# Prologue of a deformable-convolution, scan and mixture kernel: table of cells from a padded transpose, image loop unrolled

## The chip, the core and the metric

The kernel runs on one core of one Trainium2 chip. The metric is the device time of one execution in microseconds. A core has five engines with queues of their own: TensorE (PE, with its weight loads shown as PEld), VectorE (DVE), ScalarE (ACT), GpSimd (POOL) and SyncE (SP). SP, ACT and POOL also issue transfers, which run on 16 shared DMA engines.

## What is computed

The input x has 8 images of 128 channels and 64 x 64 pixels. Layer 0 normalises each image by groups of four channels, computes a 3x3 convolution with 27 outputs per pixel (nine dy, nine dx, nine masks), and samples the normalised image bilinearly at nine moved positions per pixel, weighted by the mask's sigmoid. A 128 x 128 product per tap follows.

```
om = _conv(gn(x), w_off, b_off)                 # 27 x 64 x 64 per image
dy, dx, m = om[:, :9], om[:, 9:18], sigmoid(om[:, 18:])
v = g(y0,x0)*(1-wy)*(1-wx) + g(y0,x0+1)*(1-wy)*wx + g(y0+1,x0)*wy*(1-wx) + g(y0+1,x0+1)*wy*wx
out = einsum('bckhw,ock->bohw', v * m, weight) + bias      # pixels outside the image count as 0
x = x + out
```

Layer 1 treats the pixels as 4096 tokens per image: a state-space scan over the tokens (state 256 x 256 per image) and a mixture of 8 experts with the top 2, both after a layer norm and both added to the input.

## The kernel before

The kernel has two parts. A prologue prepares tables in HBM; then a loop over the 4096 tokens of all 8 images together does everything else (sampling, projections, scan, experts). The change is in the prologue alone.

**Tables in HBM.** `table` has a row for each cell of each image. A cell is a 2 x 2 neighbourhood of pixels, of 65 x 65 per image (CELLS = 65), counting those that hang over the border; its row holds the 128 channels of its four pixels, 512 floats or 2 KB. A sample needs exactly one cell, so the main loop gathers one row per pixel and tap (line 578). `recs` holds for each pixel nine cell numbers and 36 weights. `xl` is a copy of x with a zero tail. `rz` (two of them, 8.8 MB each) holds a block structure for the scan's decays that must be zero where the loop writes nothing.

**prepare()** (lines 159 to 217) loads A, splits it in three bf16 parts, stores them in `adr`, and loads them back into `alhs` by 18 small DMAs on SP and 18 on ACT. It then clears both `rz` from a zeroed tile `zr` (lines 196 to 201), the tails of `xl` and `recs`, and the border rows and columns of the table (lines 208 to 217, 64 DMAs).

**images()** (line 228) sets up constants and runs a hardware loop `tc.For_i(0, NB, 1)` (line 268) whose body is **image()** (line 271). All engines and outstanding transfers meet at a barrier between two turns. One turn:

- loads the image into `xb` by eight DMAs, half on SP and half on ACT, with bn_stats on DVE for each, and stores it to `xl` from ACT's queue (277 to 283);
- averages over groups by two small matmuls and gets the reciprocal deviation, with a square root on ACT (287 to 298);
- writes the normalised image `xn` on DVE and copies it into the padded `xpad` (66 x 66) on POOL (305 to 314);
- transposes `xn` by 32 transposes on PE into PSUM, in 8 groups; ACT and DVE take turns to copy the groups to `xtok`, pixels on partitions (319 to 327). Each group is stored into the four corners of the cells by eight DMAs of 64 x 4 pieces of 512 bytes, SP for even image rows and ACT for odd ones (328 to 337): 64 DMAs per image, whose targets interleave in `table`;
- computes the offsets: 8 groups of 9 matmuls, 27 output partitions by 512 pixels each (341 to 351), bias on DVE into `om_t`, four transposes into `omp`, copy on ACT into `om` (352 to 359);
- computes the cell numbers and weights on DVE in some 30 operations of 128 x 288 (366 to 407), called the record chain below, and stores `recs` (408).

The pools `big` and `small` have one buffer per tile, `vp` three, and the PSUM pool `ps` two for each of its tags `pa` and `pb`. A scheduler orders the prologue's instructions on each engine at build time; each engine then works strictly in that order. A DMA instruction waits on its issuing queue for what it needs, and what stands behind it in the queue waits too.

**The main loop** (line 1106) runs 8 turns of 32 blocks in an order written out by hand. It gathers from `table`, so it starts when the prologue's stores have landed; the first thing of the main part to run on POOL is the memset of `zc` (line 450). In it, line 1020 contracts the state with 32-column weights that go to four column positions of PE in turn.

Of the kernel before, what the change touches and what calls it, by code (L numbers as in the profile page):

```python
# [37 lines left out]
PADW = IMG + 2  # L38
CELLS = IMG + 1
NCELL = CELLS * CELLS  # L40
DIN = 256
NH = 2
# [5 lines left out]
NCH = BL // CH  # L48
CT = CH * QI
GD = 14  # L50
NA = P // GD
NG = 2 * NA + 1
GCOL = (NG + 1) * CT
RROW = GD * GCOL
# [22 lines left out]
def kernel(  # L77
# [19 lines left out]
    nc = tc.nc  # L97
    NB = x.shape[0]
# [7 lines left out]
    ident = const.tile([P, P], FP, name="ident")  # L106
# [15 lines left out]
        out=wdelta_sb, in_=w_delta.rearrange("(k p) d -> p k d", p=P)  # L122
# [11 lines left out]
        out=ew_sb.rearrange("p (e c) -> p e c", e=NEXP),  # L134
        in_=expert_w.rearrange("e d c -> d e c"),
# [23 lines left out]
    def prepare():  # L159

        with tc.tile_pool(name="pre", bufs=1) as pre, tc.tile_pool(
# [45 lines left out]

            tab = table.rearrange("(b y x) (q c) -> b y x q c", x=CELLS, y=CELLS, q=4)
# [19 lines left out]
    def images():  # L228

        with ExitStack() as es:  # L230
# [32 lines left out]
            nc.sync.dma_start(out=woff_sb, in_=w_off)  # L263
            boff_sb = one.tile([27, 1], FP, name="boff_sb")
            nc.sync.dma_start(out=boff_sb, in_=b_off.unsqueeze(1))
            first = one.tile([P, 1], FP, name="first")
            nc.vector.memset(first, float(CELLS + 1))
            with tc.For_i(0, NB, 1) as b:  # L268
                image(b, big, small, vp, ps, gavg, basey, basex, woff_sb, boff_sb, first)

    def image(b, big, small, vp, ps, gavg, basey, basex, woff_sb, boff_sb, first):
        xb = big.tile([P, NPIX], FP, name="xb")
        src = x[bass.ds(b, 1)].rearrange("o c n -> c (o n)")
        stats = small.tile([P, 8, 6], FP, name="stats")
        for i in range(8):
            cols = slice(512 * i, 512 * i + 512)
            (nc.sync if i % 2 == 0 else nc.scalar).dma_start(
                out=xb[:, cols], in_=src[:, cols]
            )
            nc.vector.bn_stats(stats[:, i, :], xb[:, cols])  # L280
        nc.scalar.dma_start(
            out=xl[bass.ds(b, 1), :, :NPIX].rearrange("o c n -> c (o n)"), in_=xb
        )

# [14 lines left out]

        xpad = big.tile([P, PADW, PADW], FP, name="xpad")  # L300
        nc.gpsimd.memset(xpad[:, 0, :], 0.0)  # L301
# [3 lines left out]
        xn = big.tile([P, NPIX], FP, name="xn")  # L305
        for i in range(4):
            cols = slice(1024 * i, 1024 * i + 1024)
            nc.vector.tensor_scalar(
                xn[:, cols], xb[:, cols], gmean, grstd, ALU.subtract, ALU.mult
            )  # L310
            nc.gpsimd.tensor_copy(
                xpad[:, 1 + 16 * i : 17 + 16 * i, 1 : 1 + IMG],
                xn[:, cols].rearrange("p (y x) -> p y x", x=IMG),
            )


        tab = table.rearrange("(b y x) (q c) -> b y x q c", x=CELLS, y=CELLS, q=4)
        xtok = big.tile([P, NT, P], FP, name="xtok")
        for i in range(NT // 4):
            tp = ps.tile([P, 4, P], FP, tag="pa", name="tp")  # L320
            for k in range(4):
                t = 4 * i + k
                nc.tensor.transpose(tp[:, k, :], xn[:, P * t : P * t + P], ident)
            if i % 2 == 0:
                nc.scalar.copy(xtok[:, 4 * i : 4 * i + 4, :], tp)
            else:
                nc.vector.tensor_copy(xtok[:, 4 * i : 4 * i + 4, :], tp)
            for q in range(4):
                dy, dx = divmod(q, 2)
                for r in range(2):  # L330
                    y0 = 8 * i + r - dy + 1
                    (nc.sync if r == 0 else nc.scalar).dma_start(
                        out=tab[
                            bass.ds(b, 1), y0 : y0 + 7 : 2, 1 - dx : 1 - dx + IMG, q, :
                        ].rearrange("o y x c -> x (o y) c"),
                        in_=xtok[64 * r : 64 * r + 64, 4 * i : 4 * i + 4, :],
                    )


        om = big.tile([P, NT, 27], FP, name="om")  # L340
        for i in range(NT // 4):
            op = ps.tile([P, 512], FP, tag="pb", name="op")
            for tap in range(TAPS):
                kh, kw = divmod(tap, 3)
                nc.tensor.matmul(
                    op[:27, :],
                    woff_sb[:, tap, :],
                    xpad[:, 8 * i + kh : 8 * i + kh + 8, kw : kw + IMG],
                    start=(tap == 0),
                    stop=(tap == TAPS - 1),  # L350
                )
            om_t = vp.tile([27, 512], FP, name="om_t")
            nc.vector.tensor_scalar(om_t, op[:27, :], boff_sb, None, ALU.add)
            omp = ps.tile([P, 4, 27], FP, tag="pa", name="omp")
            for k in range(4):
                nc.tensor.transpose(
                    omp[:, k, :], om_t[:, P * k : P * k + P], ident[:27, :27]
                )
            nc.scalar.copy(om[:, 4 * i : 4 * i + 4, :], omp)

# [3 lines left out]
        def cell(base, lo, name):  # L364
# [20 lines left out]
        idxf = tmp("idxf")  # L385
        nc.vector.tensor_scalar(idxf, ylow, float(CELLS), first, ALU.mult, ALU.add)
# [21 lines left out]
        nc.sync.dma_start(  # L408
            out=recs[bass.ds(b, 1), :NPIX, :].rearrange("o (t p) x -> p (o t) x", p=P),
            in_=rec,  # L410
# [754 lines left out]
```

## Time and profile before

| what | value |
|---|---|
| median of 10 runs | 37964.98 us (37910.76 to 37986.14) |
| the profiled execution | 37936.39 us |
| its span, first to last instruction | 37934.7 us |
| granted TensorE clock, mean | 0.964 |
| busy share PE, DVE, ACT, POOL | 83%, 72%, 63%, 82% |
| memset of zc, after the last image | at 1686.56 us |
| table stores: SP queue, ACT queue | 256 and 256 DMAs, 128.0 KB each |
| row zeros (rz) | 2 DMAs of 8828.8 KB |
| PE line 345 (offsets) in one image | 144 records, 64.5 us busy |
| PE line 323 (transposes) in one image | 32 records, 6.9 us busy |

The shares of the whole span describe the main loop, which fills 95% of it. For a change in the prologue the stretches up to 1687 us have to be asked for by themselves. In the timeline, a line gives the start, the time, the engine (SPq and ACTq are their queues), the line of the kernel, the operation, what it writes and reads, and in brackets how long the engine had been idle and what ended that. A matmul in f32 shows as two records.

### The profile page before, as it was taken

Reading aid. Unit: us, or ns where it says so; the run is one execution under the profiler, and the core shown is the slowest. Engines: PE = TensorE matmul, PEld = TensorE weight load, DVE = VectorE, ACT = ScalarE, POOL = GpSimd, SP = SyncE. Lnnn points to the kernel's source line nnn. Section 1 sums busy time; section 2 is a strip of 40 time slices with the busy share of each in tenths; the row PEclk is TensorE's granted clock in tenths of the full one; section 3 lists DMA queues with packets and bytes.
Section 4 is the critical chain, followed back from the end, with each engine's and each line's share of the span. In section 5 each row is a group of like instructions: output and inputs, shape, how many; then the busy total and the mean of one; then the engine's idle time right before and its main releaser. Section 6 shows DMA issues by size and latency. Waiting matters only on the chain. (4 is left out here: it accounts for less than half of the span.)

```text
span 37934.7 us, 852122 instructions
## 1 busy us (share of the span) xinstructions
PE 31421.4 (83%) x324270; PEld 17742.7 (47%) x324270; DVE 27305.8 (72%) x35860; ACT 24041.9 (63%) x62725; POOL 31041.9 (82%) x14691
## 2 busy tenths in 40 slices
PE   3488888888888888888888888888888888888888
PEld 1144444444444444444444444444444444444444
DVE  1277777777777777777777777777777777777777
ACT  0166666666666666666666666666666666666666
POOL 0188888888888888888888888888888888888888
PEclk7799999999999999999999999999999999999999
DMA  3333333333333333333333333333333333333333
GB/s 88 76 105 105 102 105 104 104 105 105 104 102 105 104 104 104 104 105 103 105 103 104 104 104 106 101 106 106 105 103 104 105 105 104 106 102 103 105 105 99
DMA packets 4799915, 3906.86 MB, mean 103 GB/s; under 512 B 3351549, under 2 KB 4378966, under 8 KB 4536022
## 3 DMA queue, kind: packets, MB, share of 16 engines
q1 hardware_dynamic: 4529962, 3182.00, 29.6%
q0 software_dynamic: 185760, 608.85, 5.8%
q10 hardware_dynamic: 80072, 61.51, 0.6%
q8 instruction: 2532, 41.48, 0.5%
q14 instruction: 1589, 13.02, 0.1%
HBM read 3268.71 MB, written 582.10 MB: 102 GB/s over the span
## 5 line engine op out<-in xcount | busy, mean ns | idle before, releaser
L1000 POOL TENSOR_TENSOR mt<-et,ht 128x1024 f32<-128x1024 f32 x12288 | 28721.7, 2366 | 4728.5 <-ACT et L972 3435.9
L972 ACT ACTIVATE et<-bank 128x448 f32<-128x448 f32 (+1 forms) x40980 | 19926.6, 519 | 10775.4 <-PE bank L963 10457.7
L1008 DVE TENSOR_TENSOR ht<-mt,up 128x1024 f32<-128x1024 f32 x12288 | 14964.7, 1218 | 8791.7 <-PE ud L988 5499.3
L963 PE MATMUL bank<-rt,alhs 126*128 126x224 bf16 (+1 forms) x81960 | 12586.5, 254 | 2336.2 <-ACT et L972 2056.9
L963 PEld LDWEIGHTS <-alhs 126*128 126x128 bf16 x81960 | 6874.6, 99 | 7538.4 <-issue 6740.5
L1020 PE MATMUL yp<-mt,zc 128*32 128x256 f32 x98304 | 9081.9, 394 | 0.0
L988 PE MATMUL up<-uu 32*128 32x256 bf16 x49152 | 4988.4, 274 | 1972.2 <-DVE ht L1008 1935.4
L1010 DVE TENSOR_TENSOR ud<-md,ud 128x1024 f32<-128x1024 f32 x4096 | 5004.0, 1222 | 0.0
L1000 DVE TENSOR_TENSOR md<-et,ud 128x1024 f32<-128x1024 f32 x4097 | 4973.6, 1214 | 22.3 <-ACT et L972 22.3
L1020 PEld LDWEIGHTS yp<-mt,zc 128*32 128x32 f32 x98304 | 3409.6, 111 | 2790.3 <-issue 1361.1
L1020 PE MATMUL yp<-md,zc 128*32 128x256 f32 x32768 | 4650.9, 406 | 0.0
L988 PEld LDWEIGHTS <-uu 32*128 32x128 bf16 x65536 | 1789.0, 92 | 5057.6 <-issue 4427.7
L611 PE MATMUL bank<-ident,w 128*128 128x128 f32 x18576 | 3142.5, 292 | 344.8 <-ACT et L972 220.9
L601 ACT ACTIVATE w<-g,rec 128x128 f32<-128x128 f32 x9288 | 3197.2, 404 | 128.9 <-DMA rec<-recs 113.2
L611 PEld LDWEIGHTS bank<-ident,w 128*128 128x128 f32 x18576 | 2429.5, 191 | 1138.3 <-ACT et L972 542.6
L578 POOL DMA_INDIRECT g<-table,rec x2322 | 2261.5, 974 | 498.3 <-issue 245.5
L988 PE MATMUL ud<-uu 32*128 32x256 bf16 x16384 | 1605.2, 273 | 361.4 <-DVE md L1000 351.2
L1020 PEld LDWEIGHTS yp<-md,zc 128*32 128x32 f32 x32768 | 1688.6, 113 | 0.0
L896 ACT ACTIVATE se<-bank,gate 128x128 f32<-128x128 f32 x2048 | 696.2, 367 | 539.0 <-PE bank L889 486.7
L301 POOL MEMSET xpad<- 128x66 f32 x8 | 1.2, 153 | 1226.9 <-POOLq L268 1226.8
L554 PE MATMUL bank<-wconv_sb,vt 128*128 128x128 f32 x4644 | 905.8, 295 | 0.0
L554 PE MATMUL bank<-ident,se 128*128 128x128 f32 x4096 | 821.6, 306 | 0.0
(200 smaller groups left out, 16369.8 us busy)
## 6 DMA issues: line engine op xcount, KB each, us to landing
rt<-rz SPq DMA_DIRECT2D x2050, 1102.5 KB
uu<-pr SPq DMA_DIRECT2D x8196, 36.0 KB
pr<-dpt SPq DMA_DIRECT2D x3084, 48.0 KB
pr<-bpt SPq DMA_DIRECT2D x3084, 48.0 KB
rz<-dst SPq DMA_DIRECT2D x6939, 21.0 KB
g<-table,rec POOLq DMA_INDIRECT x2322, 3.5
rec<-recs SPq DMA_DIRECT2D x2064, 2.8 KB
table<-xtok SPq DMA_DIRECT2D x256, 128.0 KB
```

The costliest lines, as they stand in the source:

```text
L554: nc.tensor.matmul(ps_out, lhs, rhs, start=(i == 0), stop=(i == n - 1))
L578: nc.gpsimd.indirect_dma_start(out=g, out_offset=None, in_=table, in_offset=bass.IndirectOffsetOnAxis(ap=rec.bitcast(I32)[:, j : j + 1], a ...
L601: nc.scalar.activation(ws[j][:, P * q : P * q + P], g[:, P * q : P * q + P], AF.Copy, scale=rec[:, c0 : c0 + 1],)
L611: nc.tensor.matmul(wk[:, :P], w[:, P * q : P * q + P], ident, start=(q == 0), stop=(q == 3),)
L896: nc.scalar.activation(se[:, ex, :], wk[:, P * j : P * j + P], AF.Copy, scale=gate[:, ex : ex + 1],)
L963: nc.tensor.matmul(ps[:, m * (NH * f + h) : m * (NH * f + h + 1)].rearrange("p (q t) -> p q t", q=n), alhs[:KR, g + f, P * h : P * h + P], ...
L972: nc.scalar.activation(ec[:, :, :, P * f + d0 : P * f + d0 + n], ps[:, m * f * NH : m * (f + 1) * NH].rearrange("p (h d t) -> p h t d", h= ...
L988: nc.tensor.matmul((up if p < QP else ud)[:, r, h], uu[c % 2][rows, 0, b % 2, lo, P * h : P * h + P], uu[c % 2][rows, 1, b % 2, lo, :], st ...
L1000: (nc.gpsimd if p < QP else nc.vector).tensor_tensor(buf(j, p), et[c % 2][:, lo, PAIRS[p][0] : PAIRS[p][1] + 1 : 2], ht[p] if p < QP else ...
L1008: nc.vector.tensor_tensor(ht[p], buf(j, p), up, ALU.add)
L1010: nc.vector.tensor_tensor(ud, buf(j, p), ud, ALU.add)
L1020: nc.tensor.matmul(yp[32 * (b // 2) : 32 * (b // 2) + 32, :DIN], zc[c % 2].rearrange("p s x -> p (s x)")[:, s0 : s0 + 32], buf(j, p)[:, r, ...
```

## The change

- **Loop.** The images are unrolled: image() is called eight times with a number in place of a register, so the scheduler sees all eight and there is no barrier between them. `first`, a running offset of the cell number, becomes a constant per image.
- **Table.** The normalised image goes straight into `xpad` (two buffers now); `xn`, `xtok` and POOL's copy are gone. For each of 66 padded rows and both dx, 65 pixels are transposed on PE, so that a tile `xc` of 65 partitions (cell columns) holds for 14 padded rows the pixel pairs. Two rows that follow each other in a partition are one cell, so 13 rows of cells are stored by one DMA with an overlapping source, in pieces of 2 KB: five DMAs per image, three on SP and two on POOL. The border cells come from the padding, so their zeroing goes. An image takes 140 transposes and 35 copies of 65 x 512.
- **Offsets.** Four groups of rows go to output partitions 0, 32, 64 and 96 of one PSUM bank, tap by tap; the bias has four copies; the later transposes read at the four offsets.
- **Row zeros.** `rz` is cleared from POOL's queue by eight DMAs of 112 rows of 10 KB behind each of the first two images, from a smaller zero tile set by POOL.

```diff
+CROW = 13
...
-            zr = pre.tile([GD * 8, 9 * RROW + GCOL // 8], BF, name="zr")
-            nc.vector.memset(zr, 0.0)
-            for k in range(2):
-                nc.sync.dma_start(
-                    out=rz[k].rearrange("q (r x) -> (q r) x", r=8), in_=zr
-                )
...
-            for b in range(NB):
-                for q in range(4):
-                    dy, dx = divmod(q, 2)
-                    nc.sync.dma_start(
-                        out=tab[b, dy * IMG, :, q, :], in_=zf[:CELLS, :P]
-                    )
-                    nc.scalar.dma_start(
-                        out=tab[b, :, dx * IMG, q, :], in_=zf[:CELLS, :P]
-                    )
...
-            with tc.For_i(0, NB, 1) as b:
-                image(b, big, small, vp, ps, gavg, basey, basex, woff_sb, boff_sb, first)
+            nz = (9 * NCH * RROW + GCOL) // 64
+            zr = one.tile([GD * 8, nz], BF, name="zr")
+            nc.gpsimd.memset(zr, 0.0)
+            for b in range(NB):
+                image(b, big, small, vp, ps, gavg, basey, basex, woff_sb, boff_sb)
+                if b < 2:
+                    for m in range(8):
+                        nc.gpsimd.dma_start(
+                            out=rz[b].rearrange("q (r m x) -> (q r) m x", r=8, m=8)[:, m],
+                            in_=zr,
+                        )
...
-        xpad = big.tile([P, PADW, PADW], FP, name="xpad")
+        xpad = big.tile([P, PADW, PADW], FP, name="xpad", bufs=2)
...
             nc.vector.tensor_scalar(
-                xn[:, cols], xb[:, cols], gmean, grstd, ALU.subtract, ALU.mult
-            )
-            nc.gpsimd.tensor_copy(
                 xpad[:, 1 + 16 * i : 17 + 16 * i, 1 : 1 + IMG],
-                xn[:, cols].rearrange("p (y x) -> p y x", x=IMG),
+                xb[:, 1024 * i : 1024 * i + 1024].rearrange("p (y x) -> p y x", x=IMG),
+                gmean, grstd, ALU.subtract, ALU.mult,
             )
...
+        for i in range(CELLS // CROW):
+            xc = vp.tile([P, CROW + 1, 2, P], FP, name="xc")
+            for j in range((CROW + 1) // 2):
+                tp = ps.tile([P, 2, 2, P], FP, tag="pa", name="tp")
+                for k in range(2):
+                    for dx in range(2):
+                        nc.tensor.transpose(
+                            tp[:CELLS, k, dx, :],
+                            xpad[:, CROW * i + 2 * j + k, dx : dx + CELLS], ident,
+                        )
+                dst = xc[:CELLS, 2 * j : 2 * j + 2]
+                if j % 2 == 0:
+                    nc.scalar.copy(dst, tp[:CELLS])
+                else:
+                    nc.vector.tensor_copy(dst, tp[:CELLS])
...
+            rows = bass.AP(
+                tensor=rows.tensor, offset=rows.offset,
+                ap=[rows.ap[0], (2 * P, CROW), (1, 4 * P)],
+            )
+            r0 = NCELL * b + CROW * CELLS * i
+            (nc.sync if i % 2 == 0 else nc.gpsimd).dma_start(
+                out=table[r0 : r0 + CROW * CELLS, :].rearrange("(y x) c -> x y c", x=CELLS),
+                in_=rows,
+            )
...
-        for i in range(NT // 4):
+        for i in range(2):
             op = ps.tile([P, 512], FP, tag="pb", name="op")
             for tap in range(TAPS):
                 kh, kw = divmod(tap, 3)
...
+                for g in range(4):
+                    y0 = 32 * i + 8 * g + kh
+                    nc.tensor.matmul(
+                        op[32 * g : 32 * g + 27, :], woff_sb[:, tap, :],
+                        xpad[:, y0 : y0 + 8, kw : kw + IMG],
+                        start=(tap == 0), stop=(tap == TAPS - 1),
+                    )
...
+            for g in range(4):
+                nc.vector.tensor_scalar(
+                    om_t[32 * g : 32 * g + 27], op[32 * g : 32 * g + 27],
+                    boff_sb[32 * g : 32 * g + 27], None, ALU.add,
+                )
...
-        nc.vector.tensor_scalar(first, first, float(NCELL), None, ALU.add)
```

On the queues, as the changed kernel is scheduled: ACT's 18 loads of alhs stand ahead of the first image's square root; on SP an image's record store and the loads of the next image's `xb` stand ahead of the next image's table stores; on POOL six of the rz stores stand ahead of the first table store; on DVE and ACT the statistics of the next image and its copy to `xl` stand between the copies out of PSUM; on PE an image's first matmul stands behind the last `omp` of the image before, and on DVE its normalisation behind the record chain of the image before.

More of the change, by code (lines that the diff above doesn't have):

```diff
@@ L206, in prepare @@
                 nc.scalar.dma_start(out=recs[b, NPIX:, :], in_=zf[: 2 * BL, :REC])
-            tab = table.rearrange("(b y x) (q c) -> b y x q c", x=CELLS, y=CELLS, q=4)
-            for b in range(NB):
-                for q in range(4):
-                    dy, dx = divmod(q, 2)
-                    nc.sync.dma_start(
-                        out=tab[b, dy * IMG, :, q, :], in_=zf[:CELLS, :P]
-                    )
-                    nc.scalar.dma_start(
-                        out=tab[b, :, dx * IMG, q, :], in_=zf[:CELLS, :P]
-                    )
     def rstd_of(pool, var, shape, eps, name):
@@ L263, in images, with image @@
             nc.sync.dma_start(out=woff_sb, in_=w_off)
[L264 to L268, printed above, removed]
-                image(b, big, small, vp, ps, gavg, basey, basex, woff_sb, boff_sb, first)
-    def image(b, big, small, vp, ps, gavg, basey, basex, woff_sb, boff_sb, first):
+            boff_sb = one.tile([P, 1], FP, name="boff_sb")
+            nc.vector.memset(boff_sb, 0.0)
+            for g in range(4):
+                nc.sync.dma_start(
+                    out=boff_sb[32 * g : 32 * g + 27], in_=b_off.unsqueeze(1)
+                )
[10 more added lines that the diff above has]
+                        )
+    def image(b, big, small, vp, ps, gavg, basey, basex, woff_sb, boff_sb):
         xb = big.tile([P, NPIX], FP, name="xb")
-        src = x[bass.ds(b, 1)].rearrange("o c n -> c (o n)")
         stats = small.tile([P, 8, 6], FP, name="stats")
@@ L277, in image @@
             (nc.sync if i % 2 == 0 else nc.scalar).dma_start(
-                out=xb[:, cols], in_=src[:, cols]
+                out=xb[:, cols], in_=x[b, :, cols]
             )
             nc.vector.bn_stats(stats[:, i, :], xb[:, cols])
-        nc.scalar.dma_start(
-            out=xl[bass.ds(b, 1), :, :NPIX].rearrange("o c n -> c (o n)"), in_=xb
-        )
+        nc.scalar.dma_start(out=xl[b, :, :NPIX], in_=xb)
         mv = small.tile([P, 2], FP, name="mv")
@@ L304, in image @@
         nc.gpsimd.memset(xpad[:, 1 : PADW - 1, PADW - 1], 0.0)
-        xn = big.tile([P, NPIX], FP, name="xn")
         for i in range(4):
-            cols = slice(1024 * i, 1024 * i + 1024)
             nc.vector.tensor_scalar(
-                xn[:, cols], xb[:, cols], gmean, grstd, ALU.subtract, ALU.mult
-            )
-            nc.gpsimd.tensor_copy(
-                xpad[:, 1 + 16 * i : 17 + 16 * i, 1 : 1 + IMG],
-                xn[:, cols].rearrange("p (y x) -> p y x", x=IMG),
-            )
@@ L317, in image @@
-        tab = table.rearrange("(b y x) (q c) -> b y x q c", x=CELLS, y=CELLS, q=4)
-        xtok = big.tile([P, NT, P], FP, name="xtok")
-        for i in range(NT // 4):
[L320 to L337, printed above, removed]
+                xpad[:, 1 + 16 * i : 17 + 16 * i, 1 : 1 + IMG],
@@ new lines, in image @@
+                xb[:, 1024 * i : 1024 * i + 1024].rearrange("p (y x) -> p y x", x=IMG),
+                gmean, grstd, ALU.subtract, ALU.mult,
+            )
+        for i in range(CELLS // CROW):
[13 more added lines that the diff above has]
+                    nc.vector.tensor_copy(dst, tp[:CELLS])
+            rows = xc[:CELLS, :CROW]
+            rows = bass.AP(
+                tensor=rows.tensor, offset=rows.offset,
+                ap=[rows.ap[0], (2 * P, CROW), (1, 4 * P)],
+            )
+            r0 = NCELL * b + CROW * CELLS * i
[3 more added lines that the diff above has]
+            )
@@ L340, in image @@
         om = big.tile([P, NT, 27], FP, name="om")
-        for i in range(NT // 4):
+        for i in range(2):
             op = ps.tile([P, 512], FP, tag="pb", name="op")
@@ L344, in image @@
                 kh, kw = divmod(tap, 3)
[L345 to L350, printed above, removed]
-                )
[L352 to L359, printed above, removed]
+                for g in range(4):
[5 more added lines that the diff above has]
+                    )
+            om_t = vp.tile([P, 512], FP, name="om_t")
+            for g in range(4):
+                nc.vector.tensor_scalar(
+                    om_t[32 * g : 32 * g + 27], op[32 * g : 32 * g + 27],
+                    boff_sb[32 * g : 32 * g + 27], None, ALU.add,
+                )
+            for g in range(4):
+                omp = ps.tile([P, 4, 27], FP, tag="pa", name="omp")
+                for k in range(4):
+                    nc.tensor.transpose(
+                        omp[:, k, :], om_t[32 * g : 32 * g + 27, P * k : P * k + P],
+                        ident[32 * g : 32 * g + 27, 32 * g : 32 * g + 27],
+                    )
+                t0 = 16 * i + 4 * g
+                nc.scalar.copy(om[:, t0 : t0 + 4, :], omp)
         def tmp(name):
@@ L385, in image @@
         idxf = tmp("idxf")
-        nc.vector.tensor_scalar(idxf, ylow, float(CELLS), first, ALU.mult, ALU.add)
+        nc.vector.tensor_scalar(
+            idxf, ylow, float(CELLS), float(NCELL * b + CELLS + 1), ALU.mult, ALU.add
+        )
         nc.vector.tensor_add(idxf, idxf, xlow)
@@ L408, in image @@
         nc.sync.dma_start(
-            out=recs[bass.ds(b, 1), :NPIX, :].rearrange("o (t p) x -> p (o t) x", p=P),
+            out=recs[b, :NPIX, :].rearrange("(t p) x -> p t x", p=P),
             in_=rec,
```

## The prediction

> **What bounds the kernel now.** The profiled execution took 37936.39 us (span 37934.7); the median of the ten runs is 37964.98, 28.6 more. The sum is made against the profiled one and 28.6 is added at the end. A tenth of a per cent or two (the runs span 75 us) is all that a measurement of this kernel can tell from no change, hence the bound of 0.2% below.
>
> I read the table by stretches first. Up to 1.69 ms the profile shows another program: PE busy 37%, ACT 4%.
>
> ```profile
> 300.00:500.00 200.00, 74.56 (x212) 23.25 (x212) 30.51 (x60) 7.56 (x16) 5.94 (x8) 0.67 0.30 68
> 1300.00:1500.00 200.00, 74.47 (x212) 23.16 (x212) 33.72 (x65) 7.56 (x16) 5.95 (x8) 0.67 0.32 76
> 1900.00:2100.00 200.00, 166.50 (x1746) 92.51 (x1739) 152.21 (x211) 133.01 (x345) 174.28 (x83) 0.98 0.40 109
> ```
>
> Columns: stretch, length, busy us of PE, PE weight loads, DVE, ACT, POOL (instructions), granted clock, DMA share, GB/s. In the image loop no engine is half busy and DMA is at 0.30. So a wait bounds it: next come the waits of the SP queue in 0 to 1700 us (total us, times, longest) and the timeline of one image.
>
> ```profile
> SPq L332 <- DMA table<-xtok: 1112.3, 312, 5.5
> SPq L332 <- ACT xtok L325: 91.8, 8, 14.1
> SPq L268 <- DMA recs<-rec: 85.2, 8, 11.0
> ```
>
> ```profile
> 325.01 0.15 POOL L301 MEMSET xpad<- 128x66 f32 x1 [173.76 <-POOLq L268]
> 338.30 2.91 PE L323 MATMUL tp<-ident,xn 128*128 128x128 f32 x12 [1.53 <-DVE xn L308]
> 340.06 165.40 SPq L332 DMA_DIRECT2D table<-xtok  x32
> 414.41 0.46 DVE L367 TENSOR_TENSOR posy<-om,basey 128x288 f32<-128x288 f32 x1 [1.01 <-ACT om L359]
> 424.76 0.69 DVE L407 TENSOR_TENSOR rec<-posy,posx 128x288 f32<-128x288 f32 x1
> 1492.73 0.15 POOL L301 MEMSET xpad<- 128x66 f32 x1 [176.03 <-POOLq L268]
> 1673.15 0.44 SPq L408 DMA_DIRECT2D recs<-rec  x1
> 1686.56 1.95 POOL L450 MEMSET zc<- 128x1088 f32 x2 [175.08 <-DMA table<-xtok]
> ```
>
> Six images lie between 325.01 and 1492.73: 194.6 us each. 165.4 of it is the train of table stores: 32 on SP and 32 on ACT, each waiting for the one before (2.6 us a store), at 50 GB/s. Arithmetic ends at 425.5, 100 us into the image; the rest is the train and the loop's barrier. The scan begins when everything before it is done (1686.56) and lasts 36,248 us.
>
> **The change, part by part.** After the prologue the order of the instructions is the same on every engine, so those 36,248 us stay. What moves is 1686.56, rebuilt from three pieces.
>
> *Start, now 130 us.* Out go the memset of zr (16.88 us on DVE), the row zeros that held all DMA engines from 25 to 80 us, and 64 border stores (111.5 to 129). The 18 loads of alhs on each queue stay; SP took 15.29 us for its own undisturbed, ACT 37.7 under the row zeros. ACT's stand ahead of the first image's square root. adr can land by about 20 us, 18 loads at SP's 0.85 make 35, plus normalisation: transposes from 38. Bounds 30 (0.55 a load, ACT's median issue) and 70 (2.1, as now).
>
> *Eight images.* The train becomes five stores of 845 pieces of 2 KB (1.73 MB), none of which waits for another; xc has three buffers. SP issues three, POOL two. Bytes stay at 8.65 MB an image. What the stores cost on the engines is bounded by rows: the 2 KB loads of xb ran at 406 GB/s (21 us an image), the 512-byte border stores at 150 (58 us). I take 26, nearer to the row with the same piece size. With xb and xl (2.1 MB each, about 5 us each) and recs (about 9) transfers need 45 us an image.
>
> ```profile
> 330.00:332.00 2.00, 0.00 (x0) 0.00 (x0) 1.89 (x3) 0.00 (x0) 0.00 (x0) 0.50 1.05 406
> ```
>
> That is below the arithmetic, which now sets the period. PE's order lets an image start only after the last omp of the one before, and DVE puts the whole record chain between that and the next normalisation. One image:
> - record chain, 414.41 to 425.45: 11.0.
> - dev to the first transpose (335.71 to 338.30): 2.6.
> - 35 tiles of 4 transposes (140 for 32 before), each evicted by ACT (0.585) or DVE (0.69) from two banks, with 18 rounds of four offset matmuls between. Now two tiles and two matmul records take 2.0 us (152.60 to 154.60: eight transposes 1.09, two records 1.04). A round is eight records on four column sets; if they overlap it is 2 x 0.43, so again 2.0 a pair: 17.5 x 2.0 = 35.
> - xb has one buffer: the next load starts after the normalisation, and bn_stats on DVE and the xl store on ACT wait for it ahead of evictions, and those hold up PE. Load 8 us (326 to 334), queued beside recs, so landing about 18 us after the chain, when some 8 tiles (10.6 us) are done: 7.
> - clock: after the chain it is 0.50 and eight transposes took 1.75 for 1.09; a pair then costs 3.8, two pairs until it is warm, once more after the stall: 7.
> - DVE in order: four om_t of 0.74 ahead of an eviction, twice, less what two banks cover: 4.
> - eight omp with evictions at the end, 0.7 each: 5.5.
>
> Sum 72 us. Bounds: 51 (PE dense, no stall) and 96 (cold throughout). Costed at nothing: POOL's copies to xpad (5.4, gone), the memsets of xpad, POOL's issue of two stores (0.95 for 128 pieces of a gather, so some 6 each; behind them only memsets that are needed an image later), 8 bn_stats in the load's shadow.
>
> Do the column sets overlap? Line 1020 of the scan does the same, 32 columns at four positions:
>
> ```profile
> 20002.34 0.73 PE L963 MATMUL bank<-rt,alhs 126*128 126x224 bf16 x4
> 20003.00 1.07 PE L1020 MATMUL yp<-mt,zc 128*32 128x256 f32 x16
> 20004.00 0.56 PE L963 MATMUL bank<-rt,alhs 126*128 126x224 bf16 x4
> ```
>
> 16 records of 256 columns in 1.07 us; one by one at 0.43 per 512 columns they would take 3.4. So 64.5 us of offsets become about 16. Without it an image costs 48 more.
>
> The Trainium skill (TensorEngine Tiling (Array Packing), Key Properties) says that changing the tiling mode drains TensorE. The kernel now alternates transposes on the whole array with rounds on column sets 36 times an image. The trace above switches both ways with neighbours overlapping, so no drain shows. Were it to cost a matmul's tail (0.379 less 0.213 us, 0.17) each time, it would add 6 us an image, and the forecast would be 36,960.
>
> *Row zeros*, 17.7 MB at the 340 GB/s of 30 to 70 us: 52 us of all engines, in 16 POOL stores, now beside images 0 and 1. Those two need 90 of 144 us for their own, so together they just fit; POOL's own table store stands behind six of them in its queue, and a late one holds an xc buffer. I take 10, bounds 0 and 52.
>
> *End*: recs store to barrier, 1673.15 to 1686.56: 13. Most rec loads are then done early: 3 us less.
>
> Sum: 38 + 8 x 72 + 10 + 13 = 637, for 1686.6. Saved 1050 + 3; 37936.4 - 1053 = 36,883, and 28.6 more for the median: **36,910**.
>
> **Rivals.**
> 1. *Transfers become the bound.* With stores at 150 GB/s an image needs 58 + 19 = 77, and with stalls in bursts (three buffers, SP's stores behind rec loads that wait for recs) some 95: 8 x 23 more, 37,095. For: DMA at 0.55 when the 65-row stores ran at 150. Against: those are 32.5 KB each, on small pieces. The Trainium skill (DMA: Bandwidth & Descriptors, "How many engines (k)") says that a transfer uses the largest k up to 16 that divides its outer size; 65 rows would use 13, by which 406 becomes 330 GB/s and the stores 26 us. No run here shows the engines one by one. Chance 0.22.
> 2. *Column sets run one after another*: 120 an image, 37,295. Line 1020 speaks against it. 0.03.
> 3. *More overlap*: no stall, warm clock, 55 an image, 36,775. PE's order and the single xb are against it. 0.10.
> 4. *Slower: POOL's stores.* They are made of 845 pieces by an engine whose only transfers here are gathers of 128. If a piece costs much more in a store than there, two stores in a row set the image. The gather's landing, 3.6 us for 128, is 28 ns a piece: 24 us a store, 48 an image, hidden. It decides on the total from about 203 us an image (8 x 203 + 61 = 1686), that is 120 ns for each of 1690 pieces; at 150 ns it gives 254 an image, 38,375. Nothing in the trace comes near. 0.03.
> 5. *The change does not do what it says*: the new stores still wait for each other, 5 x about 8 us: 40 an image, hidden again; the time stays. It joins the forecast.
>
> **How the numbers follow.** Forecast 0.62 (36,800 to 37,020 by itself), rivals 0.22, 0.03, 0.10, 0.03. The range takes half of rival 3 and nearly all of rival 1: 36,780 to 37,160 (its top is 96 an image, start 70, zeros 52 less a little). Faster by over 0.2%: all but rival 4, less 0.01 for what I have not thought of, 0.96; slower 0.03; same 0.01.
>
> **What would show it.** Right: zc's memset near 640 us; image starts about 72 apart; SP's waits on its own table stores gone; the offset matmuls about 16 us busy an image; DVE waiting for xb some 7 us an image; DMA share near 0.6 in the images. Wrong: evictions waiting for a table store (rival 1), offset matmuls near 64 us (2), POOL transfers landing after more than 50 us (4), a start beyond 70, or a scan that is not 36,248 us within 0.2%.

## The result and the profile after

The change was faster: 36911.29 us median of 8 runs (36878.97 to 36929.18) against 37942.94 of 28 runs (37883.32 to 38005.75), ratio 0.9726 with a 95% interval of 0.9718 to 0.9735. The profiled execution took 36907.24 us, its span is 36902.8, and its memset of `zc`, which marks the end of the prologue, stands at 658.30 (line 452 now) instead of 1686.56. The scan behind it took 36902.8 - 658.3 = 36244.5 us, for 36248.1 before. So the whole gain, 1028 us, lies in the prologue.

The table by stretches, changed kernel, first the prologue as a whole and then the middle of the image loop (columns as before: length, busy us of PE, PE weight loads, DVE, ACT, POOL, granted clock, DMA share, GB/s):

```profile
0.00:658.00 658.00, 369.61 (x2564) 191.42 (x2564) 294.49 (x569) 134.44 (x259) 41.73 (x80) 0.80 0.80 200
300.00:500.00 200.00, 135.09 (x946) 68.66 (x946) 105.35 (x201) 46.39 (x91) 7.07 (x18) 0.80 0.85 200
```

Where DMA stood at 0.30 and 68 GB/s it now stands at 0.85 and 200. PE is at two thirds. So the DMA engines have less idle time left than any other engine, and the experiments ask what a byte more costs there.

The waits of the SP queue, 0 to 700 us:

```profile
SPq L328 <- DVE xc L319: 257.7, 21, 36.4
...
SPq L565 <- DMA recs<-rec: 61.0, 8, 28.8
```

The wait of a table store for a table store, 1112.3 us before, is not in the list. SP now waits for DVE to finish a tile, which is where it should wait.

The timeline, cut to the time around image 0 and to the end of the last image:

```profile
36.61 2.98 DVE L298 TENSOR_SCALAR xpad<-xb,gmean,g_r 128x1024 f32<-128x1024 f32 x4
36.74 3.99 POOL L261 DMA_DIRECT2D rz<-zr  x6 [0.30 <-POOL zr L256]
...
67.99 44.26 SPq L328 DMA_DIRECT2D table<-xc  x3
...
96.68 0.58 ACT L317 COPY xc<-tp 65x512 f32<-65x512 f32 x1 [21.83 <-DMA table<-xc]
...
112.31 26.83 SPq L271 DMA_DIRECT2D xb<-in_x  x4
...
166.40 2.71 DVE L274 BATCH_NORM_STATS2 stats<-xb 128x6 f32<-128x512 f32 x4 [34.23 <-DMA xb<-in_x]
...
582.15 2.98 DVE L298 TENSOR_SCALAR xpad<-xb,gmean,g_r 128x1024 f32<-128x1024 f32 x4
...
646.11 0.40 SPq L410 DMA_DIRECT2D recs<-rec  x1
...
658.30 1.95 POOL L452 MEMSET zc<- 128x1088 f32 x2 [42.53 <-DMA recs<-rec]
```

An image's time, or period, is counted below from the start of its normalisation to the start of the next one's. The eight images start their normalisation (line 298) at 36.61, 172.17, 235.51, 310.25, 380.37, 446.67, 514.76 and 582.15. Image 0 takes 135.6 us; the next six take 68.3 on average (410.0 / 6), the last 64.0 to its record store, and 12.2 follow. In image 0 the evictions wait 22 us for a table store and the statistics of image 1 wait 34 us for its load: those are the two places to ask about.

### The profile page after: what moved, and what is told of

Same layout as the page of the kernel before. It is cut to its first block, busy times and chain, and to the rows that moved or that the text cites. A ratio compares the mean times of both kernels' runs of the same rounds, so it can differ in the third digit from the quotient of the medians.

```text
span 36902.8 us, 851327 instructions
## 1 busy us (share of the span) xinstructions
PE 31218.1 (85%) x325134; PEld 17758.9 (48%) x325134; DVE 27338.0 (74%) x35939; ACT 24109.2 (65%) x62853; POOL 31010.2 (84%) x14692
## 5 line engine op out<-in xcount | busy, mean ns | idle before, releaser
L603 ACT ACTIVATE w<-g,rec 128x128 f32<-128x128 f32 x9288 | 3197.2, 404 | 43.8 <-DMA g<-table,rec 41.8
L556 PEld LDWEIGHTS bank<-wconv_sb,vt 128*128 128x128 f32 x4644 | 657.1, 190 | 263.4 <-issue 263.1
```

The lines of the kernel that those rows point to most:

```text
L556: nc.tensor.matmul(ps_out, lhs, rhs, start=(i == 0), stop=(i == n - 1))
L603: nc.scalar.activation(ws[j][:, P * q : P * q + P], g[:, P * q : P * q + P], AF.Copy, scale=rec[:, c0 : c0 + 1],)
```

## The experiments

The kernel before took 38419.49 us on the chip of the first four runs (7 runs; its granted clock there was 0.954 to 0.955, elsewhere 0.963 to 0.966), 37987.03 on that of the next four (one run) and 37929.1 on that of the last four (9 runs). So totals are compared as ratios, and prologues by the memset of `zc` in the profile.

### e1_zeros_last and e2_zeros_spread: the zeros moved in the text

```diff
-                if b < 2:
-                    for m in range(8):
...
+                if b == NB - 1:
+                    for k in range(2):
+                        for m in range(8):
...
```

That is e1, with all 16 stores behind the last image; e2 has two behind each image:

```diff
-                if b < 2:
-                    for m in range(8):
...
+                for m in range(2 * (b % 4), 2 * (b % 4) + 2):
...
```

> All 16 stores of row zeros stand behind the last image instead of eight behind each of the first two. In the changed kernel image 0 lasts 135.6 us and images 1 to 7 on average 67.7. Theory (the row zeros hold the DMA engines while image 1's load and image 0's table stores need them): image 0 takes 68 to 80 us, images 1 to 7 stay at 65 to 70, and the memset of zc, now at 658.3, comes at about 658 - 60 + 52 = 650, because the 52 us of zeros are then bare at the end. Rival (image 0 is long for its own reasons: cold clock, loads of alhs, first load of x): image 0 stays at 125 to 136 us and zc moves out to about 710.

> Two stores of row zeros (2.2 MB) behind each of the eight images. Theory (the zeros cost what they cost because 17.7 MB come at once): image 0 takes 68 to 80 us; each image carries 6.5 us more of transfers, of which the slack of some 7 us in a period of 67.7 hides most; periods of 67 to 73, zc at 595 to 630, total 30 to 60 us below the changed kernel. Rival A (image 0 long for its own reasons): image 0 at 125 to 136, zc at 655 or later. Rival B (transfers already bind, so bytes cost the same wherever they stand): periods of 74 or more, zc at 650 to 660, nothing gained.

Image 0 took 120.0 us in the first and 123.6 in the second; `zc` came at 650.9 and 654.8. The second, timed, had the ratio 0.973 (0.9714 to 0.9746), the same as the change. Read alone, that would have killed the theory. But POOL's timeline of the first shows that hardly anything had moved:

```profile
36.76 4.03 POOL L262 DMA_DIRECT2D rz<-zr  x6 [0.30 <-POOL zr L256]
...
70.46 1.07 POOL L262 DMA_DIRECT2D rz<-zr  x2
...
119.86 4.16 POOL L262 DMA_DIRECT2D rz<-zr  x8
```

The scheduler issues a store as soon as it is ready, wherever the program's text has it. The stores of zeros depend on nothing but their tile, so they went to the front in the order of the changed kernel; only the last eight came some 13 us later, from 119.86 on for 106.71. Neither run tells what zeros at another place would cost. They were repeated with the order pinned (below).

### e3_one_column_set: the offsets as before, the rest of the change kept

```diff
-        for i in range(2):
+        for i in range(NT // 4):
...
-                for g in range(4):
-                    y0 = 32 * i + 8 * g + kh
-                    nc.tensor.matmul(
-                        op[32 * g : 32 * g + 27, :], woff_sb[:, tap, :],
...
+                nc.tensor.matmul(
+                    op[:27, :], woff_sb[:, tap, :],
+                    xpad[:, 8 * i + kh : 8 * i + kh + 8, kw : kw + IMG],
...
```

> The offsets go back to eight groups of nine matmuls on one column set, the rest of the change stays. Theory (TensorE's work sets the period of an image and column sets take 43 us out of it): offsets 64.5 us busy an image instead of 21, periods of 105 to 115 us, zc at about 658 + 8 x 43 = 1000, total about 37,250. Rival (the transfers, 60 of 67 us, set the period): the longer matmuls hide partly, periods of 75 to 95, zc below 900.

Images 1 to 6 took 110.1 us (220.21 to 880.85, six periods) and `zc` came at 1002.0. The table by stretches:

```profile
500.00:600.00 100.00, 80.87 (x284) 29.74 (x283) 34.41 (x69) 15.44 (x28) 2.36 (x6) 0.88 0.52 116
```

The DMA share falls to 0.52 and PE is at 81%: the period follows TensorE's work, and column sets save 110.1 - 68.3 = 41.8 us an image. In the image from 441.39 to 550.68 the offset matmuls were busy for 68.3 us, in the changed kernel for 21.3, so only some 5 of these 47 us were hidden. TensorE in the changed kernel, where transposes of the table and offset matmuls take turns:

```profile
106.20 1.09 PE L311 MATMUL tp<-ident,xpad 128*65 128x128 f32 x8
...
107.22 1.06 PE L341 MATMUL op<-xpad,woff_sb 128*27 128x512 f32 x8
...
108.21 1.09 PE L311 MATMUL tp<-ident,xpad 128*65 128x128 f32 x8
```

Eight offset records, which one by one at 0.43 would take 3.4 us, take 1.06 on four column sets, and the whole turn takes 2.0.

### e4_old_unrolled: the old body, only unrolled

```diff
-            with tc.For_i(0, NB, 1) as b:
-                image(b, big, small, vp, ps, gavg, basey, basex, woff_sb, boff_sb, first)
+            for b in range(NB):
+                image(b, big, small, vp, ps, gavg, basey, basex, woff_sb, boff_sb, first)
```

> The image body, the border stores and the row zeros of before, but unrolled over the images in place of the hardware loop. Theory (the train of 64 table stores that wait for each other sets an image; the loop's barrier and the bare load are what unrolling takes out): 165 to 172 us an image for 194.6, zc at about 130 + 8 x 168 + 13 = 1490, total about 37,740. Rival 1 (unrolling is the main gain, and the chained waits came from the loop's form): below 120 us an image, zc below 1100. Rival 2 (nothing from unrolling, because the train of an image and the load of the next share the queues): 190 or more, zc at 1650 to 1690.

This is the run that changed the picture. `zc` came at 925.8: unrolling alone saved 1686.6 - 925.8 = 760.8 us of the 1028. The total was 37652.34 (one run, ratio 0.980). The seven periods average 97.0 us. SP's waits from 0 to 1800 us:

```profile
SPq L332 <- DMA table<-xtok: 10.0, 31, 1.0
```

and one image's stores in the timeline:

```profile
532.78 34.81 SPq L332 DMA_DIRECT2D table<-xtok  x32
```

SP's stores of 512-byte pieces, which waited 1112 us for table stores in the hardware loop, wait 10 us here, and SP issues the 32 of an image in 35 us instead of 165. The train was not a property of the stores: in an unrolled body, with a number for the image in their addresses, the waits are gone; in the hardware loop, with a register there, they are there (e5 shows the same for the new stores). Loop and register were changed together in both runs. That the build can compare only numbers for overlap is the likely reason, and it is not shown; the runs show the effect. The theory had expected the train to stay; rival 1 was right.

### e5_new_in_loop: the other half alone

```diff
-            for b in range(NB):
...
+            with tc.For_i(0, NB, 1) as b:
...
-                out=table[r0 : r0 + CROW * CELLS, :].rearrange("(y x) c -> x y c", x=CELLS),
+                out=cells[bass.ds(b, 1), CROW * i : CROW * i + CROW].rearrange("o y x c -> x (o y) c"),
```

> The new image body in the hardware loop of before, with a register for the image in every address; all row zeros behind the loop. The unrolled old body showed that its stores no longer wait for each other (10 us in all, for 1112). Theory (it is the register in the address, not the many small stores, that chains them): the five stores of an image wait one for the other again, each about 10 us from issue to landing, so that SP or POOL waits for table stores some 30 to 50 us an image, and an image takes 100 to 125 us, with the barrier and the bare load. zc at about 37 + 8 x 112 + 52 + 13 = 1000. Rival (the new stores are free of each other in any form): no such waits, and an image takes 85 to 95 us (67.7 with 8 of load, 12 of records and barrier bare), zc at about 37 + 8 x 90 + 65 = 820.

`zc` at 813.9, images 90.1 us apart, total 37022.68 (one run, ratio 0.975). The start was 75.2: image 0 is loaded inside the loop here, from 56.7 on, and the scheduler put half of the zeros ahead of the loop. The waits of SP and POOL, 0 to 650 us:

```profile
SPq L332 <- DMA table<-xc: 298.9, 13, 23.4
...
POOL table L332 <- DMA table<-xc: 66.4, 2, 33.5
```

The mechanism is the theory's: behind a register the new stores wait for each other again, 23 us at a time on SP. The price is the rival's: 90.1 us an image, so most of the chain must lie beside the arithmetic. Fewer, larger stores made the chain cheap; the unrolled loop, with numbers for addresses, made it go away.

### e10_old_table_columns: the loop and the offsets of the change, without its table and its row zeros

e4 with the offsets of the changed kernel (lines 335 to 360 there) in place of its own.

> The old image body unrolled, as in the fourth run, and the offsets on four column sets; the table stored as before by 64 stores of 512-byte pieces. In the fourth run an image took 97 us, with the offsets 64.5 us of TensorE and the transfers at a share of 0.55, some 54 us. Theory (unrolling and column sets are the gain, the new table form is not): 97 - 43 = 54 us of arithmetic with 54 us of transfers, stalls between them, 60 to 72 us an image; first normalisation at 142 as there, zc at about 142 + 7 x 66 + 70 = 675. Rival (the new table form is needed: 64 stores on two queues hold up the evictions on ACT and the transfers): 85 us an image or more, zc above 800.

Normalisations at 143.32, 201.71, 268.74, 333.34, 401.40, 466.74, 531.69 and 597.26: 64.8 us an image, averaged over seven. `zc` at 666.4, total 36901.42 (one run, ratio 0.971). With a start that is 107 us later than the changed kernel's it ends its prologue only 8 us later. The late start is the old one: the row zeros are issued from 24.67, the border stores from 111.38, and the images begin behind both. So what the change does to table and row zeros gave the early start and, with four column sets, hardly anything else. The four runs with numbers for addresses make a square (its first row also has the row zeros where they were before):

| `zc` at (first normalisation at) | one column set | four column sets |
|---|---|---|
| old table | 925.8 (142.6) | 666.4 (143.3) |
| new table | 1002.0 (37.7) | 658.3 (36.6) |

On one column set `zc` even comes 76 us later with the new table, in spite of the early start: an image takes 110.1 us for 97.0, and its 140 transposes keep TensorE busy for 22 us where the 32 old ones took 6.7.

### e1b_zeros_pinned_last and e2b_zeros_pinned_spread: the zeros really moved

```diff
+                    tc.keep_in_program_order(nc.gpsimd.dma_start(
                         out=rz[...].rearrange("q (r m x) -> (q r) m x", r=8, m=8)[:, m],
                         in_=zr,
+                    ))
```

> The row zeros pinned behind the last image's stores in POOL's order. (In the first two runs the scheduler had put six of the 16 ahead of the first table store, two behind it and eight behind image 0, whatever the text said, as in the changed kernel.) Theory (the zeros make image 0 long): image 0 at 68 to 85 us, images 1 to 7 at 65 to 70, zc at 635 to 660, the zeros bare at the end. Rival (image 0 is long for its own reasons: loads of alhs ahead of the table stores on SP, cold clock): image 0 at 115 or more, zc at 690 or later.

> Two stores of row zeros pinned behind the table stores of each image in POOL's order. Theory (the zeros' 52 us of transfers cost that much because they come at once; 6.5 us fit into an image's slack of some 7): image 0 at 70 to 85 us, the others at 67 to 72, zc at 590 to 625. Rival A (transfers bind, so that every byte costs its time anywhere): periods of 74 or more, zc at 645 to 665, as in the changed kernel. Rival B (image 0 long for its own reasons): image 0 at 115 or more, zc at 640 or later.

| zeros | image 0 | images 1 to 6, mean | last normalisation to `zc` | `zc` |
|---|---|---|---|---|
| ahead and beside images 0, 1 (the change) | 135.6 | 68.3 | 76.1 | 658.3 |
| all behind image 7 (e1b) | 82.5 | 69.7 | 139.1 | 678.9 |
| two behind each image (e2b) | 90.6 | 74.6 | 89.3 | 666.5 |

The theory on image 0 held: without the zeros it takes 82.5, so the zeros cost 53 us there. Its hope for a free place did not. Behind the last image they cost 63; spread, they cost 4.9 to 6.3 us in each period (74.6, for 69.7 in e1b or 68.3 in the change), with 2.2 MB of transfers added, 6.5 us at 340 GB/s. That is rival A of the second run, though `zc` came 1.5 us after the end of its range. The end of e1b in the table by stretches:

```profile
600.00:700.00 100.00, 16.09 (x95) 14.63 (x95) 14.64 (x33) 15.82 (x55) 20.45 (x25) 0.57 0.76 219
620.00:650.00 30.00, 0.00 (x0) 0.00 (x0) 0.00 (x0) 0.00 (x0) 2.62 (x5) 0.50 0.98 299
```

PE 16%, DMA 0.76 over a stretch that includes the first 21 us of the scan; from 620 to 650 no other engine than POOL works, and the zeros move with the last of the image's stores. They go in pieces of 10 KB, at 299 GB/s and a share of 0.98. The 340 GB/s of the prediction were measured on pieces of 40 KB, so at the lower rate 17.7 MB would be some 59 us of transfers (an estimate) and not 52, which accounts for most of the 63. Neither place hides them: the images leave too little idle time on the DMA engines.

### e6_split_64_1: are 13 engines the limit of a store of 65 rows?

```diff
+            for p0, p1 in ((0, IMG), (IMG, CELLS)):
+                part = xc[p0:p1, :CROW]
...
+                eng.dma_start(out=cells[p0:p1], in_=part)
```

> Each table store of 65 partitions becomes one of 64 and one of a single partition; nothing else differs from the changed kernel. Where only table stores move, the share of the DMA engines stood at 0.82 (13/16 is 0.81) with 192 to 205 GB/s. Theory (a store of 65 rows uses 13 of 16 engines): those stretches go to a share near 1 and 235 to 245 GB/s, an image's transfers fall by some 7 us, zc at 605 to 635. Rival (writing to memory is limited at some 200 GB/s whatever the engines: the old form with 64 rows and pieces of 512 bytes also averaged 200): the same 195 to 205 GB/s, zc at 645 to 665.

Stretches of four microseconds in which little but table stores moves, one fence for the changed kernel, one for this run, one for the old form of the stores (e10b, below):

```profile
492.00:496.00 4.00, 2.85 (x23) 2.01 (x20) 3.40 (x5) 1.23 (x3) 0.92 (x1) 1.00 0.81 201
```

```profile
477.00:481.00 4.00, 4.00 (x40) 1.21 (x36) 2.44 (x5) 1.16 (x2) 0.00 (x0) 1.00 0.92 197
494.00:498.00 4.00, 4.00 (x37) 1.29 (x39) 0.00 (x0) 0.98 (x2) 0.00 (x0) 1.00 0.96 197
498.00:502.00 4.00, 3.04 (x26) 1.49 (x18) 2.44 (x4) 0.58 (x1) 0.00 (x0) 1.00 0.93 203
```

```profile
377.00:381.00 4.00, 4.00 (x40) 1.25 (x36) 0.39 (x2) 0.59 (x1) 0.00 (x0) 1.00 1.02 271
```

The first stretch has nearly SP's stores alone, and so has 477 to 481; 494 to 498 has POOL's alone, the next one both. Like for like, on SP, the share rose from 0.81 to 0.92 and the rate stayed at 197 to 201 GB/s; on POOL and on both it is 0.93 to 0.96 at 197 to 203. So no single queue is the limit either. The rival was right that engines were not the limit, and wrong that 200 is the limit of writing: the old stores, in pieces of 512 bytes, reach 271. What holds the new form at 200 was not found. By the Trainium skill (DMA: Bandwidth & Descriptors, "How many engines (k)") a transfer of 65 rows uses 13 engines; 13/16 is 0.81, and the share of 0.81 that the split lifts agrees with it. The time it would give does not follow.

The run's own prologue was longer, `zc` at 681.0 with periods of 61.2, 86.1, 60.7, 85.7, 60.6 and 85.1 us. TensorE waited 117.2 us in three waits for the next image's statistics (100 to 600 us); that the scheduler orders the queues otherwise when the stores double in number is likely, not shown. The time of this run therefore does not price the split; its rate does.

### e7c_xb_two_buffers: a second buffer for the image

```diff
-        xb = big.tile([P, NPIX], FP, name="xb")
+        xb = big.tile([P, NPIX], FP, name="xb", bufs=2)
```

> xb gets two buffers; nothing else differs from the changed kernel. Theory (transfers bind the prologue: the pinned zeros cost their 52 us or more wherever they stood): the wait for xb goes away on DVE and comes back as waits for table stores, images 1 to 7 at 65 to 69 us, zc at 645 to 662. Rival (the wait for xb, some 8 us an image, is bare time): 58 to 61 us an image, zc at 600 to 615.

Images 1 to 6 took 68.3 us, `zc` came at 665.1, the total was 36934.68 (one run, ratio 0.974). The number is the theory's, the reason is not shown, since the wait did not go away: DVE still waited 37.6 us for loads of `xb` in 235 to 580, for 46.5 in the changed kernel. The timeline around image 4, whose normalisation begins at 390.54:

```profile
322.79 11.81 SPq L271 DMA_DIRECT2D xb<-in_x  x4
...
389.19 0.37 DVE L279 BATCH_NORM_AGGREGATE mv<-stats 128x2 f32<-128x48 f32 x1
...
393.55 8.29 SPq L271 DMA_DIRECT2D xb<-in_x  x4
...
404.77 1.29 DVE L274 BATCH_NORM_STATS2 stats<-xb 128x6 f32<-128x512 f32 x2 [6.13 <-DMA xb<-in_x]
```

The load at 393.55 is not the next image's. Image 5 was loaded from 322.79 on, behind image 3's normalisation, and its statistics were complete at 389.19, before image 4 was normalised. What starts at 393.55, when DVE has read image 4, is the load of image 6 into the buffer that image 4 leaves. The second buffer moved every load one image ahead, and DVE's order moved the statistics ahead with it, so DVE waits for a load behind each normalisation as before, only for another image's. So this run does not decide between transfers and arithmetic.

### e10b_old_table_free_start and e9b_all_together: better versions

e10b is e10 with the border stores of an image pinned behind its record store and the row zeros pinned behind the last image:

```diff
             for b in range(NB):
                 image(b, big, small, vp, ps, gavg, basey, basex, woff_sb, boff_sb, first)
+                for q in range(4):
+                    dy, dx = divmod(q, 2)
+                    tc.keep_in_program_order(nc.sync.dma_start(
+                        out=tab[b, dy * IMG, :, q, :], in_=zf
+                    ))
+                    tc.keep_in_program_order(nc.scalar.dma_start(
+                        out=tab[b, :, dx * IMG, q, :], in_=zf
+                    ))
...
```

e9b is the changed kernel with the split, two buffers of `xb`, zeros spread and pinned, and in the program's text the next image's load, statistics and normalisation ahead of this image's record chain:

```diff
             for b in range(NB):
...
+                next(now)
+                ahead = begin(b + 1) if b + 1 < NB else None
+                for _ in now:
+                    pass
...
```

Here `next(now)` writes the tiles and offsets of image b, `begin(b + 1)` the load, statistics and normalisation of the next, and the loop over `now` the records of image b.

> The old image body unrolled, with four column sets, as in the run of that name; the border stores of an image are pinned behind its record store and the row zeros behind the last image, so that the start is no longer held until 143 us. Theory (bytes set the time: the same 127 MB at 200 GB/s, only the idle start is saved): first normalisation at 37 to 50, images at 64 to 69 us, the zeros bare at the end, zc at 610 to 640, ratio to before 0.971 to 0.973. Rival (the 64 small border stores and the zeros give the start back): zc at 655 or later, ratio 0.973 or more.

> The changed kernel with zeros pinned two behind each image, table stores split in 64 and 1 partitions, two buffers for xb, and the front of the next image (load, statistics, normalisation) placed in the program ahead of the record chain of this one. Theory (transfers bind at some 200 GB/s whatever the order): zc at 640 to 670, ratio 0.972 to 0.974. Rival 1 (13 of 16 engines bind, and the split frees them): 127 MB at 236 GB/s are 536 us, zc at 570 to 605, ratio 0.970 to 0.9715. Rival 2 (the serial chain of an image binds, and the overlap frees it): zc below 600 with the store rate still near 200.

| | ratio to before (95%) | median us (runs) | `zc` | scan (span less `zc`) | granted clock |
|---|---|---|---|---|---|
| the change | 0.9726 (0.9718 to 0.9735) | 36911.29 (8) | 658.3 | 36244.5 | 0.972 |
| e10b | 0.9692 (0.9679 to 0.9706) | 36761.0 (5) | 614.9 | 36144.4 | 0.976 |
| e9b | 0.9696 (0.9682 to 0.9709) | 36792.14 (5) | 625.9 | 36166.5 | 0.976 |

By these ratios both are faster than before and than the change. In the prologue e10b went much as its theory had it (first normalisation at 39.06, 63.5 us an image, just under the 64 to 69 expected, `zc` at 614.9). e9b ended at 625.9, between its theory's 640 and its rivals' 605. The ratios of both lie below every range that was expected, for a reason outside the prologue. e9b from 100 to 200 us:

```profile
100.00:200.00 100.00, 50.28 (x363) 27.47 (x362) 48.14 (x104) 22.37 (x45) 5.55 (x16) 0.73 1.00 208
```

The DMA engines have no idle time left there, and they move 208 GB/s; from 300 to 500 us the share is 0.95. The overlap is there, and in that stretch the transfers bind.

The prologue explains 43 and 32 us of the lead over the change. By the ratios the leads are about 0.0034 x 37,940 = 129 and 0.0030 x 37,940 = 114 us. The rest lies in the scan, whose loop has the same instructions in the same order in all of them. The clock in the table is that of the whole execution, prologue included (0.964 for the kernel before, whose long prologue ran at some 0.68). Over the scan alone, in the profiled executions, the length goes with the granted clock: 36295.4 at 0.9740 (e2b), 36244.5 at 0.9756 (the change), 36248.1 at 0.9763 (before), 36155.8 at 0.9793 (e6), 36144.4 at 0.9803 (e10b), and 36702 to 36739 at 0.965 to 0.967 on the chip of the first four runs. In the five executions of e10b the clock of the whole was 0.974 to 0.977, in the change's 0.971 to 0.974. What decides this was not found, neither whether it is the kernel or the chip, so no more than those 43 and 32 us are claimed for the edits.

## Why the prediction was right, and where it was not

The time was right: 36,910 forecast, 36,911 measured. It is partly luck, as the terms show.

| term | forecast | measured |
|---|---|---|
| start | 38 | 36.6 |
| eight images without zeros | 576 (72 each) | 556.5 = 82.5 (e1b's image 0) + 410.0 + 64.0 |
| row zeros | 10 (0 to 52) | 53.1 = 135.6 - 82.5 |
| end | 13 | 12.2 |
| `zc` | 637 | 658.4 (658.3 in the profile) |

- **The start** was right: with zeros, border stores and DVE's big memset gone from it, transposes began at 37.48.
- **An image's period** was 3.7 us too long for images 1 to 6. In image 5 the record chain took 11 us (502.2 to 512.9) for 11.0, dev to the first transpose 2.8 for 2.6, the tiles and offsets 50 for 53 (35, the stall of 7, the cold 7 and the ordered 4), with the wait for `xb` (8.7 on DVE) among them, and the last omp 4 for 5.5. The pair of tiles did take 2.0 us (eight transposes 1.09, eight offset records 1.06).
- **Column sets overlap**, as read from line 1020. The offsets of an image are 21 us busy, not 16; the clock averages 0.80 in the images, by which 16 would become 20. The 48 us forecast for their lack was 41.8 (e3). The drain at a change of tiling mode (the Trainium skill, TensorEngine Tiling (Array Packing), Key Properties) does not show: a pair with two changes still takes 2.0 us, and the 6 us an image are not there.
- **The row zeros** are the term that was mis-sized. "Those two need 90 of 144 us for their own, so together they just fit; ... I take 10": the 90 rested on table stores at 26 us an image. They run at 189 to 201 GB/s, so 8.65 MB take some 44, and an image's own transfers fill about 0.85 x 68 = 58 of 68 us, not 45 of 72. With so little room, the zeros cost 53. The bound of 52, at which they cost their full transfer time, was the better guide than the value taken, though it was priced at the 340 GB/s of larger pieces (e1b).
- **The store rate** was put nearer to the 2 KB loads (406 GB/s) than to the 512-byte stores (150), by piece size. The direction was the point: a store is not priced by a load of the same pieces. So the DMA share stood at 0.85 and not near 0.6, and the sentence that arithmetic alone sets the period was too strong. Within the stores, piece size ordered them the wrong way round, 2 KB at 200 and 512 bytes at 271 GB/s.
- **Rival 1** (transfers become the bound) was therefore half true: the transfers nearly bind, and bytes added to an image cost most of their time or all of it (e2b). Its sign is there too, evictions that wait for a table store: 32.8 us on ACT and 14.8 on DVE from 170 to 650. But the period is 68 and not 95: at 200 GB/s for 150 the stores take 44 us for 58, and these waits come to at most 7 us an image.
- **Rivals 2, 4 and 5** did not happen. Rival 3 (more overlap, 55 us an image) did not happen in the change; e9b has more overlap and still takes 72.8 us for images 1 to 6, with two stores of zeros in each.
- **What the prediction left out**: it credited the end of the train to the new stores, "none of which waits for another". e4 shows that the old ones would not have waited either once the loop was unrolled, and e5 that the new ones do wait inside it. The sum was not touched, but the reason was: of 1028 us, 761 come from unrolling alone and 259 to 344 from column sets, while the new table and the moved zeros give the 107 us of an earlier start and lose 99 of them again (e10). The new table was not needed even for that: e10b keeps the old one, moves the border stores and zeros behind the images, and ends its prologue 43 us earlier than the change.
- **The median**: 28.6 us were added to the profiled time, as before; after the change the median was 4.1 above it. With the prologue 21 late, the two about cancelled.

## What to carry to other kernels

A train of transfers that wait for each other may come from the loop they stand in and the register in their addresses, not from the transfers; unroll the loop alone before rewriting what is in it. In a prologue that moved 200 GB/s at a DMA share of 0.85, bytes cost about their transfer time wherever they stood: moving 17.7 MB about within it gained nothing (`zc` at 658, 679 and 667). Where a scheduler places the instructions, moving a transfer in the text is no experiment until the timeline shows that it moved.

## What was not expected of the hardware

- Stores in 2 KB pieces from 65 or 64 partitions ran at 197 to 203 GB/s (e6 and the change) whether the DMA share was 0.81 or 0.96; stores in 512-byte pieces from 64 partitions ran at 269 to 271 at a share of 1.0 (e10b, 373 to 381 us). A higher share of the same engines bought nothing. What limits the first form is open.
- The scan, the same instructions in the same order, took 36,144 to 36,295 us with its granted clock between 0.9803 and 0.9740 (36,702 to 36,739 at 0.965 to 0.967 on the chip of e1 to e4), and ten executions of the change stayed at 0.971 to 0.974 where five of e10b stayed at 0.974 to 0.977. What sets it is open.
